# Half as many turned columns a chunk, and degrees summed by VectorE: a graph layer on one core

## The chip, the core and the metric

The kernel runs on one core of one Trainium2 chip. The time is the device time of one execution in microseconds (us). Engines are called as in the profile: PE is TensorE's matmul, PEld its weight load, DVE is VectorE, ACT is ScalarE, POOL is GpSimd, SP is SyncE (here it only issues DMAs).

## What is computed

A message-passing layer over a graph of 12500 nodes (48 features) and 400000 edges (32 features), the edges sorted by `dst`:

```
h   = relu(layernorm(x))
tmp = concatenate([h[dst], h[src], edge_attr], axis=1)
m   = relu(tmp @ W1 + b1) @ W2 + b2
out = x + segment_sum(m, dst)
```

The product with W1 is split by rows of W1: `A = h @ W1[:48] + b1` and `B = h @ W1[48:96]` are computed once for all nodes and become two tables in HBM, `tab_a` and `tab_b`; table B is also kept in SBUF turned over, `bt` (128 hidden values on the partitions, one column a node). An edge then needs `relu(A[dst] + B[src] + edge_attr @ W1[96:])`. W2 and b2 are applied after the sum over edges, so the sum carries two things a node: the summed hidden rows, and the node's degree (how many edges it has), by which b2 is multiplied.

## The kernel before, in words

`node_tables` makes the tables. `windows` then walks over 391 chunks of 1024 edges, each 8 tiles of 128 edges. Since edges are sorted, the destinations of a chunk lie in a window of 80 nodes. For chunk c:

- `prepare` (L338): SP loads 80 rows of table A (`rhs`, L344), the edge features (`lhs` rows 80 to 111, L349) and the destinations, spread over 80 partitions (`row`, L351). POOL gathers rows of table B by `src`, one indirect DMA for each tile of 128 edges (L358), into `gb`, a ring of 6 buffers: POOL may be up to six chunks ahead, and waits for `hid` of the chunk whose buffer it reuses. DVE compares destinations with the window's nodes: `lhs` (L365, 80 nodes by 1024 edges) and `hot` (L370, 128 edges by 8 times 80 nodes).
- `before` (L383): PE multiplies `lhs` by `rhs`, 8 products into `pre` in PSUM: A[dst] plus the part of the edge features.
- `columns` (L336): not all B rows are gathered. For 361 of the 390 full chunks the last tile's 128 rows are copied as columns out of `bt` into a tile `gt`, one instruction for each edge, its address from a register. DVE copies 59 columns a chunk and ACT 60, in parts (PARTS: 23, 20, 16 on DVE, 28, 32 on ACT), and each part's registers are loaded by one instruction (L300) that stands ahead of it. `turned` (L393): PE multiplies `gt` by the identity, which adds the turned tile to `pre`.
- `hidden`: DVE adds `gb` to `pre` (L401, 7 tiles, or 8 where none is turned); ACT applies relu (L403 for the turned tile straight from PSUM, L404 for the others).
- `fold` (L412): PE multiplies `hid` by `hot`, 8 products that accumulate the 80 nodes' sums in `p_g`; then 8 bf16 products of a matrix with one column of ones by the upper halves of `hot` (L417) accumulate the degrees.
- `add` (L431): DVE adds `p_g` to the segment's accumulator `seg`; every twelfth chunk begins a new segment (`segment_next`: two memsets L447 and a copy L449), and `segment_sum` and `segment_store` bring old segments through W2 (L457 to L459) to the output.

The order is written out by hand (the loop at the end of `windows`). In step c, PE does `before(c-1)`, `fold(c-2)`, `turned(c-1)`; DVE does the comparisons of c with three parts of columns, `hidden(c-1)`, then `add(c-2)`; ACT does a part of columns, the relus of c-1, and another part. Every engine works through its instructions in this order and waits on semaphores.

Of the kernel before, what the change touches and what calls it, by code (L numbers as in the profile page):

```python
# [11 lines left out]
ALU = mybir.AluOpType  # L12
# [46 lines left out]
BASE = 120  # L59

BT0 = 16512
SEG0 = 121952
# [3 lines left out]
SEG, NEXT, SEG2 = 124, 125, 126  # L66
PLACE0 = 127
WIDTH = 128
# [10 lines left out]
BYCOLS = tiles_of(COLS, PART)  # L79
EPS = 1e-5  # L80
# [151 lines left out]
def windows(nc, tc, gp, bt, ident, idx, x_t, tab_a, tab_b, dst, edge_t, w1, w2s, b2s, out_t):  # L232


    srci, rel, bw, wrow, last, ones = idx
    with ExitStack() as es:
# [5 lines left out]
        gtp = es.enter_context(tc.tile_pool(name="gtp", bufs=3))  # L242
# [81 lines left out]
        def columns(c, part):  # L324

            dve, first, _, _ = PARTS[part]
            copy = nc.vector.tensor_copy if dve else nc.scalar.copy
            for k, at in enumerate(regs.pop((c, part), [])):
                j, e = divmod((c - COLS) * PART + first + k, P)
                of = BYCOLS[j]  # L330
# [5 lines left out]
                copy(gts[of][:, e : e + 1], bt8[:, bass.ds(at, 4)].bitcast(F32))  # L336

        def prepare(c):  # L338
# [18 lines left out]
            for t in range(n - (c in BYCOLS)):  # L357
# [6 lines left out]

            nc.vector.tensor_scalar(  # L365
                lhs[:W, : n * P], row[:, : n * P], bw[:, c : c + 1], None, op0=ALU.is_equal,
            )
            columns(c, 0)
# [5 lines left out]
            load(c, 1)  # L374
            st[c].update(rhs=rhs, lhs=lhs, gb=gb, hot=hot)

        def before(c):
# [4 lines left out]
            for t in range(n):  # L382
                nc.tensor.matmul(  # L383
                    pre[:, t, :], s["lhs"][:K, t * P : (t + 1) * P], s["rhs"][:K, :],
                    start=True, stop=c not in BYCOLS or t < n - 1,
                )
            s["pre"], s["added"] = pre, n - (c in BYCOLS)

        def turned(c):

            if c in BYCOLS:
                s = st[c]
                nc.tensor.matmul(  # L393
                    s["pre"][:, s["n"] - 1, :], gts.pop(c), ident, start=False, stop=True
                )

        def hidden(c):
            s = st[c]
            n, m, pre = s["n"], s["added"], s["pre"]
            h = wp.tile([P, T, HID], F32, name="hid")  # L400
            nc.vector.tensor_add(h[:, :m, :], pre[:, :m, :], s["gb"][:, :m, :])  # L401
            if m < n:
                nc.scalar.activation(h[:, m, :], pre[:, m, :], AF.Relu)  # L403
            nc.scalar.activation(h[:, :m, :], h[:, :m, :], AF.Relu)  # L404
            s["h"] = h

        def fold(c):
# [7 lines left out]
            high = s["hot"].bitcast(BF16)  # L415
            for t in range(n):
                nc.tensor.matmul(  # L417
                    p_g[:, 1, :], ones, high[:, t, 1::2], start=t == 0, stop=t == n - 1
                )
# [45 lines left out]
        with tc.manual_schedule():  # L465
            for c in range(NCH + 2):
                if c < NCH:
                    prepare(c)
                if c >= NCH:
                    columns(c, 0)  # L470
                columns(c, 1)
                load(c, 2)
                columns(c, 2)
# [24 lines left out]
                load(c + 1, 3)  # L498
# [133 lines left out]
def tile_gnn_preln(  # L632
# [55 lines left out]
    ones = const.tile([P, P], BF16, name="ones")  # L688
    nc.gpsimd.memset(ones, 0.0)
    nc.gpsimd.memset(ones[:, :1], 1.0)  # L690
# [77 lines left out]
    with tc.If(outside == 0) as cmp:  # L768
        windows(nc, tc, gp, bt, ident, (srci, rel, bw, wrow, last, ones), x_t, tab_a, tab_b, dst16, edge_t,
# [71 lines left out]
```

## Time and profile before

| what | value |
|---|---|
| time, median of 3 runs | 4973.62 us (4969.75 to 4973.76) |
| the profiled execution's own time | 4973.7 us |
| its span, first to last instruction | 4972.0 us |
| mean granted TensorE clock | 0.644 |
| busy: PE, PEld, DVE, ACT, POOL | 65%, 58%, 59%, 59%, 54% |
| instructions in the span | 94216 |
| gathers on POOL | 2764 |
| columns copied by ACT, by DVE | 23280, 22928 |
| first and last `hid` addition on DVE | 159.3 us, 4959.4 us |

How to read the rows: in the groups of instructions, a row gives the line, engine, operation, what it writes and reads, its count, then busy time in all and the mean of one in ns, then the idle time of the engine just ahead of it and what ended that. In a timeline a row gives start and duration in us, and in brackets the idle time of the engine ahead of it and what ended it: "issue" is a wait for nothing that the profile shows, "remote" a wait that ended with an event from elsewhere that could not be told. "x15" are 15 instructions merged. Register loads are not counted as busy. 391 chunks end between 159.3 and 4959.4 us, about 12.3 us each.

### The profile page before, as it was taken

The numbers are of one execution on the slowest core, as the hardware profiler recorded it, in microseconds if no ns is written. First come the engines' busy times: TensorE is split into PE (matmuls) and PEld (weight loads), VectorE is DVE, ScalarE is ACT, GpSimd is POOL, SyncE is SP. The second block draws the span as 40 slices with busy tenths as digits, with TensorE's granted clock in tenths as the row PEclk, the third lists the DMA queues.
The fourth block names the chain that finished last, engine by engine and source line by source line (L and its number), as shares of the span: only waits on it lengthen the run. The fifth ranks groups of instructions, "written<-read, shape, count | busy, mean of one in ns | idle before, by whom it ended". The sixth has DMA issues, their size and how long they took to land.

```text
span 4972.0 us, 94216 instructions
## 1 busy us (share of the span) xinstructions
PE 3217.5 (65%) x16917; PEld 2903.8 (58%) x16917; DVE 2921.8 (59%) x24741; ACT 2925.2 (59%) x24107; POOL 2704.3 (54%) x2791
## 2 busy tenths in 40 slices
PE   6666766666666666666665666666666666666666
PEld 4556655555555555566565556565555655655555
DVE  4555555555566555556565555655555555555555
ACT  3456656655566556556566555656555556555565
POOL 5355555555555555555555555555555555555553
PEclk7666666666666666666666666666666666666666
DMA  3422222222222222222222222222222222222221
GB/s 128 134 65 73 69 69 67 69 64 72 69 69 67 69 65 74 68 68 68 68 66 71 69 69 67 69 69 69 67 69 67 69 69 68 69 69 67 69 68 49
DMA packets 192085, 353.66 MB, mean 71 GB/s; under 512 B 65282, under 2 KB 97428, under 8 KB 190196
## 3 DMA queue, kind: packets, MB, share of 16 engines
q0 software_dynamic: 88480, 181.34, 14.5%
q1 hardware_dynamic: 102736, 166.09, 11.2%
q14 instruction: 470, 3.85, 0.3%
q8 instruction: 139, 2.28, 0.2%
q10 hardware_dynamic: 260, 0.10, 0.0%
HBM read 327.81 MB, written 22.07 MB: 70 GB/s over the span
## 4 chain that ended last, share of the span: by engine, by line
issue 37%; DVE 24%; POOL 21%; ACT 8%; PE 3%; DVEq 3%; DMA 2%; another core or an unknown queue 1%; ACTq 1%; SPq 0%; POOLq 0%
POOL gb L358 21%; DVE gt L336 14%; ACT gt L336 7%; DVE hid L401 3%; DVE lhs L365 3%; DVEq L300 3%; DVE hot L370 2%; DMA gb<-tab_b,srci 1%; ACT hid L404 1%; PE p_g L412 1%; PE p_n L178 1%; PE pre L383 1%; ACTq L300 1%; DVE seg L431 1%
## 5 line engine op out<-in xcount | busy, mean ns | idle before, releaser
L358 POOL DMA_INDIRECT gb<-tab_b,srci x2764 | 2682.8, 971 | 2202.5 <-DVE hid L401 1438.1
L336 ACT COPY gt<-bt 128x1 f32 x23280 | 2476.5, 187 | 1843.6 <-issue 1817.5
L336 DVE COPY gt<-bt 128x1 f32 x22928 | 1708.5, 143 | 1715.5 <-issue 1634.7
L412 PE MATMUL p_g<-hot,hid 128*128 128x80 f32 x6250 | 1397.0, 415 | 1618.9 <-ACT hid L404 1409.7
L412 PEld LDWEIGHTS p_g<-hot,hid 128*128 128x128 f32 x6250 | 1315.0, 320 | 1702.2 <-ACT hid L404 1481.3
L383 PEld LDWEIGHTS pre<-rhs,lhs 112*128 112x128 f32 x6250 | 1155.9, 285 | 99.1 <-issue 85.9
L383 PE MATMUL pre<-rhs,lhs 112*128 112x128 f32 x6250 | 1177.3, 368 | 16.7 <-DVE lhs L365 16.7
L401 DVE TENSOR_TENSOR hid<-pre,gb 128x896 f32<-128x896 f32 (+1 forms) x391 | 426.7, 1091 | 7.8 <-issue 6.7
L404 ACT ACTIVATE hid<-hid 128x896 f32<-128x896 f32 (+1 forms) x391 | 369.9, 946 | 33.6 <-DVE hid L401 33.2
L393 PE MATMUL pre<-ident,gt 128*128 128x128 f32 x722 | 278.0, 488 | 64.3 <-remote 57.5
L365 DVE TENSOR_SCALAR lhs<-row,bw 80x1024 f32<-80x1024 int16 x391 | 310.5, 794 | 12.6 <-DMA row<-in_dst 7.6
L370 DVE TENSOR_TENSOR hot<-wnum,rel 128x640 f32<-128x640 f32 x391 | 315.9, 808 | 0.8 <-issue 0.7
L417 PEld LDWEIGHTS <-ones 128*128 128x128 bf16 x3125 | 292.8, 154 | 0.0
L417 PE MATMUL p_g<-hot,ones 128*128 128x80 bf16 x3125 | 284.5, 266 | 0.0
L431 DVE TENSOR_TENSOR seg<-seg,p_g 128x160 f32 x391 | 125.8, 322 | 196.1 <-DVE hid L401 185.1
L393 PEld LDWEIGHTS pre<-ident,gt 128*128 128x128 f32 x722 | 193.0, 327 | 70.2 <-remote 62.0
L403 ACT ACTIVATE hid<-pre 128x128 f32<-128x128 f32 x361 | 97.1, 269 | 71.2 <-DVE hid L401 68.7
L457 PE MATMUL p_f<-seg,w2s 128*48 128x512 f32 (+1 forms) x134 | 122.0, 1012 | 0.4 <-DVE seg L431 0.4
L458 PE MATMUL p_f<-seg,b2s 1*48 1x512 f32 (+1 forms) x134 | 101.9, 851 | 0.0
L458 PEld LDWEIGHTS p_f<-seg,b2s 1*48 1x48 f32 x134 | 13.6, 149 | 101.6 <-issue 101.6
L447 DVE MEMSET seg<- 128x944 f32 x64 | 54.1, 845 | 9.3
L459 DVE TENSOR_TENSOR xseg<-xseg,p_f 48x512 f32<-48x512 f32 (+1 forms) x67 | 44.8, 669 | 21.6 <-PE p_f L458 21.5
(66 smaller groups left out, 298.1 us busy)
## 6 DMA issues: line engine op xcount, KB each, us to landing
row<-in_dst SPq DMA_DIRECT2D x390, 160.0 KB
lhs<-in_edge_t SPq DMA_DIRECT2D x390, 128.0 KB
gb<-tab_b,srci POOLq DMA_INDIRECT x2764
rhs<-tab_a SPq DMA_DIRECT2D x391, 40.0 KB
xseg<-in_x_t SPq DMA_DIRECT2D x33, 192.0 KB
out_x<-xseg SPq DMA_DIRECT2D x33, 192.0 KB
tab_b<-tab SPq DMA_DIRECT2D x3, 1280.0 KB
tab_a<-tab SPq DMA_DIRECT2D x3, 1280.0 KB
```

The source lines that it names most:

```text
L300: got += nc.values_load_multi_w_load_instructions(last[c % P : c % P + 1, c // P, at + k : at + min(k + MOST, n)], engines=[engine], min_v ...
L336: copy(gts[of][:, e : e + 1], bt8[:, bass.ds(at, 4)].bitcast(F32))
L358: nc.gpsimd.indirect_dma_start(out=gb[:, t, :], out_offset=None, in_=tab_b[:, :], in_offset=bass.IndirectOffsetOnAxis(ap=srci[:, c * T + t ...
L365: nc.vector.tensor_scalar(lhs[:W, : n * P], row[:, : n * P], bw[:, c : c + 1], None, op0=ALU.is_equal,)
L370: nc.vector.tensor_tensor(hot[:, :n, :], wnum.unsqueeze(1).to_broadcast([P, n, W]), rel[:, c * T : c * T + n].unsqueeze(2).to_broadcast([P ...
L383: nc.tensor.matmul(pre[:, t, :], s["lhs"][:K, t * P : (t + 1) * P], s["rhs"][:K, :], start=True, stop=c not in BYCOLS or t < n - 1,)
L393: nc.tensor.matmul(s["pre"][:, s["n"] - 1, :], gts.pop(c), ident, start=False, stop=True)
L401: nc.vector.tensor_add(h[:, :m, :], pre[:, :m, :], s["gb"][:, :m, :])
L404: nc.scalar.activation(h[:, :m, :], h[:, :m, :], AF.Relu)
L412: nc.tensor.matmul(p_g[:, 0, :], s["h"][:, t, :], s["hot"][:, t, :], start=t == 0, stop=t == n - 1)
L417: nc.tensor.matmul(p_g[:, 1, :], ones, high[:, t, 1::2], start=t == 0, stop=t == n - 1)
L431: nc.vector.tensor_add(to, to, s["p_g"])
```

## The change

The number of columns goes from 119 to 63 a chunk: 31 on DVE (parts of 15 and 16) and 32 on ACT (16 and 16). So 191 tiles instead of 361 come out of `bt`, at most one a chunk still (the code can now also place two in a chunk, which does not occur with 63), and POOL's gathers go from 2764 to 2934. `gt` has 5 buffers instead of 3. The parts stand at other places of the step: the second DVE part comes after `hidden` and `add`, and its registers are loaded ahead of `add`. The degrees: DVE's comparison into `lhs` also writes the sum of its 1024 results for each of the 80 nodes into column 0 of a tile `deg` (three of them, otherwise zero), and PE turns that by one fp32 product with the identity, in place of the 8 bf16 products.

```
-    (True, 0, 23, 1), (True, 23, 20, 24), (True, 43, 16, 44),
-    (False, 59, 28, 60), (False, 87, 32, 88),
+    (True, 0, 15, 1),
+    (True, 15, 16, 16),
+    (False, 31, 16, 32),
+    (False, 47, 16, 48),
...
-        gtp = es.enter_context(tc.tile_pool(name="gtp", bufs=3))
+        gtp = es.enter_context(tc.tile_pool(name="gtp", bufs=5))
...
-            for t in range(n - (c in BYCOLS)):
+            for t in gathered_at(c):
...
+            deg = degs[c % 3]
             nc.vector.tensor_scalar(
-                lhs[:W, : n * P], row[:, : n * P], bw[:, c : c + 1], None, op0=ALU.is_equal,
-            )
+                lhs[:W, : n * P], row[:, : n * P], bw[:, c : c + 1], None,
+                op0=ALU.is_equal, op1=ALU.add, accum_out=deg[:, :1],
+            )
+            load(c, 0)
             columns(c, 0)
...
-            high = s["hot"].bitcast(BF16)
-            for t in range(n):
-                nc.tensor.matmul(
-                    p_g[:, 1, :], ones, high[:, t, 1::2], start=t == 0, stop=t == n - 1
-                )
+            nc.tensor.matmul(p_g[:, 1, :], s["deg"], ident[:W, :W], start=True, stop=True)
...
-                columns(c, 3)
+                columns(c, DVE_PARTS)
+                for part in range(DVE_PARTS + 1, BEHIND):
+                    load(c, part)
+                    columns(c, part)
                 if 0 <= c - 1 < NCH:
                     hidden(c - 1)
-                load(c + 1, 0)
-                load(c, 4)
-                columns(c, 4)
+                if DVE_PARTS > 1:
+                    load(c, DVE_PARTS - 1)
+                for part in range(BEHIND, len(PARTS)):
+                    load(c, part)
+                    columns(c, part)
+                load(c + 1, DVE_PARTS)
                 if 0 <= c - 2 < NCH:
                     add(c - 2)
                     if k == GQ - 1:
                         segment_next(g)
-                load(c + 1, 3)
+                if DVE_PARTS > 1:
+                    columns(c, DVE_PARTS - 1)
```

DVE, one chunk in the middle of the loop before, from one `hid` on; TENSOR_LOAD is the load of a part's registers, DMASW are the semaphores of POOL's gathers, DMAHW those of SP's loads:

```order
L401 TENSOR_TENSOR hid<-pre,gb 128x896 [waits DMASW4_49,DMASW3_49,DMASW5_49,DMASW2_49,DMASW6_49,DMASW0_49,DMASW7_49,PE_49,Activation_49]
L300 TENSOR_LOAD last
L431 TENSOR_TENSOR seg_659<-seg_659,p_g 128x2x80 [waits DVE_49]
L365 TENSOR_SCALAR lhs<-row,bw 80x1024 [waits DMAHW4_49]
L336 COPY gt<-bt 128x1 [waits Activation_49]
L336 COPY gt<-bt 128x1 x22
L370 TENSOR_TENSOR hot<-wnum,rel 128x640
L300 TENSOR_LOAD last
L336 COPY gt<-bt 128x1 x20
L300 TENSOR_LOAD last
L336 COPY gt<-bt 128x1 x16
```

DVE, the same stretch of the changed program, up to the next `hid`:

```order
L426 TENSOR_TENSOR hid<-pre,gb 128x896 [waits DMASW4_49,DMASW2_49,DMASW5_49,DMASW1_49,DMASW6_49,DMASW0_49,DMASW7_49,PE_49,Activation_49]
L317 TENSOR_LOAD last
L456 TENSOR_TENSOR seg_663<-seg_663,p_g 128x2x80 [waits DVE_49]
L352 COPY gt<-bt 128x1 x16
L382 TENSOR_SCALAR lhs,deg_90<-row,bw 80x1024 [waits DMAHW6_49,DMAHW1_49]
L317 TENSOR_LOAD last
L352 COPY gt<-bt 128x1 x15
L389 TENSOR_TENSOR hot<-wnum,rel 128x640
```

From one `hid` to the next there are 31 copies instead of 59 and two register loads instead of three; `lhs` stands behind 16 copies instead of directly behind `seg`, and between `hot` and the next `hid` no copies are left.

PE in the changed program, in the middle of the loop: two chunks, the second of which has a turned tile:

```order
L441 MATMUL p_g<-hot,hid 128x80 [waits PE_49,Activation_49]
L441 MATMUL p_g<-hot,hid 128x80 x7
L444 MATMUL p_g<-ident,deg_88 128x80
L401 MATMUL pre<-rhs_707,lhs 128x128 [waits DMAHW4_49,DMAHW5_49,DVE_49,PE_49]
L401 MATMUL pre<-rhs_707,lhs 128x128 x7
L441 MATMUL p_g<-hot,hid 128x80 [waits PE_49,Activation_49]
L441 MATMUL p_g<-hot,hid 128x80 x7
L444 MATMUL p_g<-ident,deg_90 128x80
L410 MATMUL pre<-ident,gt 128x128 [waits DVE_49]
```

Before, at the place of L444 stood eight pairs of a weight load and a product (L417), and the product with the identity (L393, now L410) followed in 361 chunks; now it follows in 191. A `hid` of a chunk without a turned tile waits for the products L401 of its chunk only; with one it waits for L410, which stands behind the `fold` of the chunk before.

More of the change, by code (lines that the diff above doesn't have):

```diff
@@ L373, in prepare @@
             )
-            load(c, 1)
-            st[c].update(rhs=rhs, lhs=lhs, gb=gb, hot=hot)
+            st[c].update(rhs=rhs, lhs=lhs, gb=gb, deg=deg, hot=hot)
         def before(c):
@@ L768, in tile_gnn_preln @@
     with tc.If(outside == 0) as cmp:
-        windows(nc, tc, gp, bt, ident, (srci, rel, bw, wrow, last, ones), x_t, tab_a, tab_b, dst16, edge_t,
+        windows(nc, tc, gp, bt, ident, (srci, rel, bw, wrow, last, degs), x_t, tab_a, tab_b, dst16, edge_t,
                 w1, w2s, b2s, out_t)
```

69 lines of the change are left out of this document (43 added, 26 removed).

## The prediction

> **What bounds the kernel now.** I read the page's engines and costliest groups first, then timelines of whole chunks, then start and end of the run. The page:
>
> ```profile
> span 4972.0 us, 94216 instructions
> PE 3217.5 (65%) x16917; PEld 2903.8 (58%) x16917; DVE 2921.8 (59%) x24741; ACT 2925.2 (59%) x24107; POOL 2704.3 (54%) x2791
> ...
> L358 POOL DMA_INDIRECT gb<-tab_b,srci x2764 | 2682.8, 971 | 2202.5 <-DVE hid L401 1438.1
> L336 ACT COPY gt<-bt 128x1 f32 x23280 | 2476.5, 187 | 1843.6 <-issue 1817.5
> L336 DVE COPY gt<-bt 128x1 f32 x22928 | 1708.5, 143 | 1715.5 <-issue 1634.7
> L412 PE MATMUL p_g<-hot,hid 128*128 128x80 f32 x6250 | 1397.0, 415 | 1618.9 <-ACT hid L404 1409.7
> ```
>
> No engine is full. PE waits for ACT, POOL for DVE's `hid` (1438 us), and DVE and ACT lose 1635 and 1818 us ahead of column copies to "issue", which names no culprit. A timeline of one chunk shows what that is:
>
> ```profile
> 2506.52 1.08 DVE L401 TENSOR_TENSOR hid<-pre,gb 128x896 f32<-128x896 f32 x1
> 2507.87 0.94 POOL L358 DMA_INDIRECT gb<-tab_b,srci  x1 [3.74 <-DVE hid L401]
> ...
> 2509.12 1.02 POOL L358 DMA_INDIRECT gb<-tab_b,srci  x1 [0.30 <-issue]
> 2509.25 1.46 DVE L336 COPY gt<-bt 128x1 f32 x23
> 2509.75 2.73 ACT L336 COPY gt<-bt 128x1 f32 x28 [0.86 <-issue]
> ...
> 2512.85 0.16 DVE L336 COPY gt<-bt 128x1 f32 x1 [0.28 <-issue]
> ...
> 2513.57 0.21 DVE L336 COPY gt<-bt 128x1 f32 x2 [0.56 <-issue]
> ...
> 2514.98 0.28 ACT L336 COPY gt<-bt 128x1 f32 x2 [0.52 <-issue]
> 2514.98 0.28 DVE L336 COPY gt<-bt 128x1 f32 x3 [1.20 <-issue]
> 2515.45 0.94 POOL L358 DMA_INDIRECT gb<-tab_b,srci  x1 [0.30 <-issue]
> ...
> 2517.87 1.00 DVE L336 COPY gt<-bt 128x1 f32 x15 [0.55 <-issue]
> 2517.87 2.23 ACT L336 COPY gt<-bt 128x1 f32 x23 [0.52 <-issue]
> 2518.28 0.33 SPq L344 DMA_DIRECT2D rhs<-tab_a  x1
> 2518.78 1.08 DVE L401 TENSOR_TENSOR hid<-pre,gb 128x896 f32<-128x896 f32 x1
> ...
> 2520.14 1.22 POOL L358 DMA_INDIRECT gb<-tab_b,srci  x1 [3.74 <-DVE hid L401]
> ```
>
> At first 23 copies take 1.46 us on DVE (63 ns each) and 28 take 2.73 us on ACT (98 ns). From about 2512.5 both engines go on only at common instants 0.71 us apart, one to three copies at each; at 2517.87 both run freely again, and only then do SP and `hid` proceed. I call this the **held stretch** and its end the release. It belongs to the gathers: they start 1.25 us apart, and the release comes 2517.87 - 2515.45 = 2.42 us after the start of the last. A chunk with eight gathers moves it by the same:
>
> ```profile
> 279.36 0.95 POOL L358 DMA_INDIRECT gb<-tab_b,srci  x1 [0.30 <-issue]
> ...
> 281.81 1.67 ACT L336 COPY gt<-bt 128x1 f32 x17 [1.12 <-issue]
> 281.94 1.09 DVE L401 TENSOR_TENSOR hid<-pre,gb 128x896 f32<-128x896 f32 x1 [1.31 <-issue]
> ```
>
> Here it is 2.45 us after. And after the last gather of all, with as many columns as ever, the chunks shrink (the first row is the first `hid` of the run):
>
> ```profile
> 159.29 1.22 DVE L401 TENSOR_TENSOR hid<-pre,gb 128x1024 f32<-128x1024 f32 x1
> ...
> 4915.47 0.95 POOL L358 DMA_INDIRECT gb<-tab_b,srci  x1 [0.30 <-issue]
> ...
> 4919.81 1.22 DVE L401 TENSOR_TENSOR hid<-pre,gb 128x1024 f32<-128x1024 f32 x1
> ...
> 4927.49 1.08 DVE L401 TENSOR_TENSOR hid<-pre,gb 128x896 f32<-128x896 f32 x1
> ```
>
> 7.68 us instead of 12.26 (2506.52 to 2518.78). So columns alone do not set the pace. What the stretch does to work that needs several engines in turn is seen at the start, where POOL fills its six buffers without a pause, up to 106.9 us, while the tables are made:
>
> ```profile
> 79.19 1.35 PEld L178 LDWEIGHTS p_n<-wa,ht 97*128 97x128 f32 x4 [2.21 <-issue]
> ...
> 88.05 0.59 ACT L187 COPY tab<-p_n 128x512 f32<-128x512 f32 x1 [12.47 <-remote]
> 88.69 1.35 PEld L178 LDWEIGHTS p_n<-wa,ht 97*128 97x128 f32 x4 [8.14 <-issue]
> ...
> 99.26 0.69 DVE L185 COPY tab<-p_n 128x512 f32<-128x512 f32 x1 [20.18 <-remote]
> ...
> 105.91 0.95 POOL L358 DMA_INDIRECT gb<-tab_b,srci  x1 [0.30 <-issue]
> ```
>
> PE's products with the weights loaded from 79.19 on (done near 81 us) reach ACT at 88.05, 7 us late; the next set, done near 91, reaches DVE at 99.26. In a held stretch word of PE's work arrives late, mostly at the release. The main loop agrees (PE's wait for the columns ends at a release):
>
> ```profile
> 2617.74 2.33 ACT L336 COPY gt<-bt 128x1 f32 x24 [0.51 <-issue]
> ...
> 2617.80 0.80 PE L393 MATMUL pre<-ident,gt 128*128 128x128 f32 x2 [6.48 <-remote]
> ```
>
> So a chunk of before is a ring: release, 0.91 us of leftover copies (2517.87 to 2518.78), `hid`, 1.36 us to the first gather (2518.78 to 2520.14), six steps of 1.25, 2.42 to the release: 0.91 + 1.36 + 7.50 + 2.42 = 12.19 us, against 12.26 seen. **The bound is POOL's run with its held stretch, plus what DVE still does between release and `hid`.**
>
> **The change part by part.** Rows for the prices:
>
> ```profile
> L447 DVE MEMSET seg<- 128x944 f32 x64 | 54.1, 845 | 9.3
> ...
> L401 DVE TENSOR_TENSOR hid<-pre,gb 128x896 f32<-128x896 f32 (+1 forms) x391 | 426.7, 1091 | 7.8 <-issue 6.7
> ...
> L365 DVE TENSOR_SCALAR lhs<-row,bw 80x1024 f32<-80x1024 int16 x391 | 310.5, 794 | 12.6 <-DMA row<-in_dst 7.6
> ...
> L417 PE MATMUL p_g<-hot,ones 128*128 128x80 bf16 x3125 | 284.5, 266 | 0.0
> ```
>
> Columns: 28 fewer a chunk on each engine save 28 x 63 ns = 1.8 us on DVE and 28 x 98 ns = 2.7 us on ACT where they run freely. On the path lies only what stood behind the release. By the order DVE had 66 instructions a chunk (59 copies, 3 register loads, `lhs`, `hot`, `hid`, `seg`) and now has 37. I take it that all copies are done when the release comes, so release to `hid` shrinks from 0.91 to the semaphore's way alone: 0.4 us (2518.28 - 2517.87 = 0.41, SP's first DMA behind the same release). A gain of 0.5 us; bounds 0 and 0.9.
>
> Gathers: 2934 against 2764, 7.50 a chunk instead of 7.07: 0.43 x 1.25 = +0.54 us a chunk, 170 x 1.25 = 212 us in all if each run still starts behind a `hid`.
>
> Degrees on PE: 284.5 us / 391 = 0.73 us a chunk go, one fp32 product comes. Its weight load and product are like those of L393 (two passes in 0.80 us, quoted above), so 0 to 0.8 us. PE's idle 1619 us ahead of L412 hide either; I count 0.
>
> Degrees on DVE: `lhs` now also accumulates. It takes 794 ns for 1024 elements a partition; `hid` takes 1091 ns for 896. At `hid`'s pace 1024 elements cost 1.25 us, and the sum may need a small operation like a copy (143 ns). So 0.8 to 1.4 us; I take 1.3, nearest to `hid`'s row: +0.5 us a chunk, behind `hid`, covered by the wait for the next release (DVE's free work from `hid` on: 1.1 + 0.3 + 1.0 + 1.3 + 0.9 + 0.8, about 5.5 us with the way between them). Without that cover it costs 385 x 0.5 = 190 us. The Trainium skill speaks to this: the page "SBUF — State Buffer", section "Who interferes with whom", says that a `tensor_scalar` that also writes out its accumulator is not among the operations that can take the two-port modes. By that page `lhs` loses its doubled rate, which the upper bound above already holds; no run here shows the accumulating form.
>
> The turned chunks: with 191 of 390 turned, about every second chunk's `hid` needs no L410, so it does not wait for `fold` of the chunk before. This is what I think decides. Behind a release at 0 `hid(c-1)` starts at 0.4, the next gathers at 1.76, and DVE gets to `hid(c)` at about 6. In the chunk above, copies ran freely until about 2512.5, 4.6 us behind the first gather; so 6 us is within a few instructions of the free time. If chunk c has no turned tile, its products L401 ran early and nothing holds `hid(c)`: it runs inside the stretch, and at the next release POOL starts at once, without the 0.4 + 1.36. A turned chunk's `hid` needs `fold` and L410, whose word comes with a release.
>
> So chunks go in pairs: 0.4 + 1.36 for the first run, 0.25 for the second, two tails of 2.42, and 15 gathers less two ends, 13 x 1.25 = 16.25: **23.10 us a pair, 11.55 a chunk.** New segments (two memsets of 845 ns, 32 times) fall into DVE's slack. Larger `gt` rings and the moved parts take nothing from the path: SP's loads run three chunks ahead.
>
> The sum, against the profiled execution's 4973.7 us (the median of 4973.62 is the same): the first `hid` is at 159.3 and stays. The 385 chunks up to the last gather give 385 x 11.55 = 4447. Behind `hid` at 4919.81 come 53.9 us of six ungathered chunks; fewer copies make it about 50. Together 159 + 4447 + 50 = **4656, say 4660 us.**
>
> **The rivals.** First, longer runs: word of the early `hid(c)` gets out of the stretch before POOL finishes its chunk. POOL then does 15 gathers in one run: 0.4 + 1.36 + 14 x 1.25 + 2.42 = 21.68 a pair, 385 x 10.84 + 209 = 4380. For it: `hid(c)` is near the start of the held stretch. Against: a release at the start of the run took 7 us and more.
>
> Second, gathers back to back: DVE and ACT with half the copies no longer hold POOL at all: 7.50 x 1.25 = 9.38 a chunk, 385 x 9.38 + 209 = 3820. The Trainium skill would have it so: the page "SBUF — State Buffer", section "Who interferes with whom", states that DMA never contends with a compute engine and that PE and ACT never wait on anyone. By that rule fewer copies would simply leave POOL as the bound; here the trace disagrees, with copies at 0.71 us instants under gathers and 7.68 against 12.26 us a chunk. Against it stands the start of the run, where unbroken gathers made steps of 10 us.
>
> Third, slower: no `hid` gets ahead, since the stretch catches DVE before it (after about 4.6 us of gathers, when 15 copies, `hot` and `hid` are still to do). Then each chunk pays all: 0.4 + 1.36 + 6.50 x 1.25 + 2.42 = 12.31, and new segments still cost 32 x 1.7 = 54 us: 159 + 385 x 12.31 + 54 + 50 = 5002. The extra gathers (+0.54) eat what the leftover copies gave back (-0.5). It decides where DVE reaches `hid(c)` later than about 6 us behind the release; `lhs` at 1.4 us pushes that way.
>
> That the change does not do what it says: the order shows 31 copies between two `hid` and 7 or 8 gathers, so I give this nothing.
>
> **How the numbers follow.** Pairs 0.40; longer runs 0.23; back to back 0.09; each chunk alone 0.28, of which I put 0.20 above 4984 us, 0.05 within 0.2% and 0.03 below. (0.2%, 10 us, is about what a measurement of this kernel can tell from no change.) Faster: 0.40 + 0.23 + 0.09 + 0.03 = 0.75; same 0.05; slower 0.20. The range reaches from 50 us below the longer runs (4330) to 5050, the third rival with 0.1 us a chunk more; left out are the back-to-back case and the far ends of the others, near 0.2. The likeliest case's own range is 4570 to 4760 (`lhs`, 0.25 and 0.4 us, each off by their size).
>
> **What the profile after would show.** Pairs: `hid` at alternating distances, one of each two behind a release and one inside the held stretch; POOL's waits for `hid` about half of 381; 7- and 8-gather runs with a gap of about 1.7 us between the two of a pair and 3.3 between pairs. Longer runs: 15 gathers at 1.25 us. Back to back: POOL near all its span. Alone: 381 waits as before. `lhs` should stand near 1.25 us, with DVE idle ahead of `hid`. Wrong would be the whole account if the held stretch vanished with fewer copies, or if copies were slow without gathers.

## The result, and the profile after

The changed kernel took 4986.68 us (median of 14 runs) against 4973.53 us before (14 runs): a ratio of **1.0023, 95% interval 1.0015 to 1.0032**. The forecast was 4660 us. The time lies inside the forecast's range, but it is slightly slower, where faster was forecast.

The experiments came in five sets, each on one chip with its own runs of the kernel before (D and E on the same chip). In three of them the kernel before took about 3630 us instead of 4900 to 4974, and the traces taken in these sets show no held stretch ("the hold" from here on) in any kernel:

| set | kernel before, us | changed kernel, ratio | held stretch |
|---|---|---|---|
| first (the result) | 4973.5 | 1.0023 (1.0015 to 1.0032) | yes |
| A | 3627.8 | not run | no |
| B | 4961.4 | 1.0010 (1.0000 to 1.0020) | yes |
| C | 4902.2 | not run | yes |
| D | 3631.5 | 1.0332 (1.0315 to 1.0350) | no |
| E | 3628.8 | not run | no |

So each ratio below is to the kernel before of its own set. With the hold the change costs 0.1 to 0.2%; without it, it costs 3.3%.

The page of the changed kernel (first set), rows that answer to those of before:

```profile
span 4988.6 us, 67352 instructions
PE 2965.4 (59%) x14234; PEld 2653.0 (53%) x14234; DVE 2250.1 (45%) x14235; ACT 1953.8 (39%) x13073; POOL 2803.0 (56%) x2962
...
L374 POOL DMA_INDIRECT gb<-tab_b,srci x2934 | 2781.4, 948 | 2128.4 <-DVE seg L456 1055.6
L352 ACT COPY gt<-bt 128x1 f32 x12416 | 1497.5, 188 | 2227.8 <-issue 2206.5
...
L456 DVE TENSOR_TENSOR seg<-seg,p_g 128x160 f32 x391 | 123.3, 315 | 1609.9 <-remote 1366.0
...
L382 DVE TENSOR_SCALAR_CACHE_REDUCE lhs<-row,bw 80x1024 f32<-80x1024 int16 x391 | 495.0, 1266 | 57.9 <-issue 48.2
...
L444 PE MATMUL p_g<-ident,deg 80*128 80x80 f32 x782 | 218.1, 359 | 173.2 <-issue 171.0
```

More than a quarter of all instructions are gone, and DVE and ACT have 670 and 970 us less to do, yet ACT loses more time to "issue" than before (2207 us against 1818), and a new wait of 1366 us stands ahead of DVE's `seg`, whose row was, before:

```profile
L431 DVE TENSOR_TENSOR seg<-seg,p_g 128x160 f32 x391 | 125.8, 322 | 196.1 <-DVE hid L401 185.1
```

A timeline of one pair of chunks in the same run shows where (start, duration; in brackets the idle time ahead and what ended it):

```profile
2657.17 0.64 DVE L352 COPY gt<-bt 128x1 f32 x9 [1.24 <-issue]
...
2657.72 0.81 DVE L389 TENSOR_TENSOR hot<-wnum,rel 128x640 f32<-128x640 f32 x1
...
2658.45 1.08 DVE L426 TENSOR_TENSOR hid<-pre,gb 128x896 f32<-128x896 f32 x1
...
2659.80 0.94 POOL L374 DMA_INDIRECT gb<-tab_b,srci  x1 [5.48 <-DVE seg L456]
...
2663.26 0.39 PE L444 MATMUL p_g<-ident,deg 80*128 80x80 f32 x2
...
2663.49 1.21 DVE L426 TENSOR_TENSOR hid<-pre,gb 128x1024 f32<-128x1024 f32 x1
2663.55 0.94 POOL L374 DMA_INDIRECT gb<-tab_b,srci  x1 [0.30 <-issue]
2664.11 0.19 ACT L352 COPY gt<-bt 128x1 f32 x1 [0.53 <-issue]
...
2667.66 1.06 ACT L433 ACTIVATE hid<-hid 128x1024 f32<-128x1024 f32 x1 [0.44 <-issue]
...
2672.72 3.49 PE L441 MATMUL p_g<-hot,hid 128*128 128x80 f32 x15 [7.25 <-remote]
...
2676.91 0.32 DVE L456 TENSOR_TENSOR seg<-seg,p_g 128x160 f32 x1 [12.21 <-remote]
...
2677.15 1.05 DVE L352 COPY gt<-bt 128x1 f32 x16
2677.29 0.94 POOL L374 DMA_INDIRECT gb<-tab_b,srci  x1 [0.30 <-issue]
...
2681.08 0.76 DVE L352 COPY gt<-bt 128x1 f32 x11 [1.23 <-issue]
...
2681.76 0.81 DVE L389 TENSOR_TENSOR hot<-wnum,rel 128x640 f32<-128x640 f32 x1
...
2682.49 1.08 DVE L426 TENSOR_TENSOR hid<-pre,gb 128x896 f32<-128x896 f32 x1
...
2683.84 0.94 POOL L374 DMA_INDIRECT gb<-tab_b,srci  x1 [5.61 <-DVE seg L456]
```

The chunk without a turned tile has its `hid` 5.04 us behind the other one (2663.49), and POOL goes on without a pause (0.30 us): 15 gathers in one run, 2659.80 to 2677.29. Split where POOL stood idle for more than 1 us, the 2934 gathers make 217 runs, and 169 of them are such fifteens. In the meantime DVE stands at `seg` for 12.21 us. This `seg` adds the chunk before, whose last PE product (L444) was done at 2663.65, but the trace has the update of PE's semaphore at 2676.88, 13 us later. The fold of the chunk without a turned tile waits in the same way: ACT's relu ended at 2668.72, and PE goes on at 2672.72. The release comes at 2681.08, **3.79 us** after the last gather's start, and DVE then still has 11 copies and `hot` to do, 1.41 us to `hid` (2682.49); at the release ahead of this pair (2657.17) it was **1.28 us**. The sum is 1.28 + 1.35 + 14 x 1.25 + 3.79 = 23.9 us a pair, 12.0 a chunk. The mean of all chunks is 12.35 (first `hid` 158.3, last 4976.1, 390 steps); it holds the new segments and the chunks that go alone as well. Over the whole run the tail after the last gather is 3.81 us (median of 156 runs of 15 in which ACT's copies show the release) and release to `hid` 1.49; in the kernel before they were 2.39 and 0.85 (356 runs of 7).

Set against before: 12.31 us a chunk were 7.07 gathers of 1.25 us (8.84) and 3.47 us between them; 12.35 us are 7.50 gathers (9.38) and 2.97 us between them. **Half a microsecond saved, half a microsecond of gathers added.**

### The profile page after: what moved, and what is told of

Read it like the earlier page. It is cut to its first block, busy times and chain, and to the rows that moved or that the text cites. A ratio compares the mean times of both kernels' runs of the same rounds, so it can differ in the third digit from the quotient of the medians.

```text
span 4988.6 us, 67352 instructions
## 1 busy us (share of the span) xinstructions
PE 2965.4 (59%) x14234; PEld 2653.0 (53%) x14234; DVE 2250.1 (45%) x14235; ACT 1953.8 (39%) x13073; POOL 2803.0 (56%) x2962
## 4 chain that ended last, share of the span: by engine, by line
PE 37%; another core or an unknown queue 26%; issue 17%; DVE 13%; DVEq 2%; ACT 1%; ACTq 0%; DMA 0%; POOL 0%
PE p_g L441 16%; PE pre L401 14%; DVE gt L352 5%; DVE lhs L382 3%; PE p_g L444 2%; DVE hot L389 2%; DVEq L317 2%; DVE hid L426 2%; PE pre L410 2%; PE p_f L483 2%; PE p_f L482 1%; DVE seg L456 1%; ACT gt L352 1%; ACTq L317 0%
## 5 line engine op out<-in xcount | busy, mean ns | idle before, releaser
L374 POOL DMA_INDIRECT gb<-tab_b,srci x2934 | 2781.4, 948 | 2128.4 <-DVE seg L456 1055.6
L352 ACT COPY gt<-bt 128x1 f32 x12416 | 1497.5, 188 | 2227.8 <-issue 2206.5
L441 PE MATMUL p_g<-hot,hid 128*128 128x80 f32 x6250 | 1259.1, 379 | 1442.2 <-remote 915.6
L441 PEld LDWEIGHTS p_g<-hot,hid 128*128 128x128 f32 x6250 | 1195.4, 291 | 1459.5 <-remote 948.2
L401 PE MATMUL pre<-rhs,lhs 112*128 112x128 f32 x6250 | 1231.7, 377 | 112.3 <-issue 81.6
L401 PEld LDWEIGHTS pre<-rhs,lhs 112*128 112x128 f32 x6250 | 1172.1, 287 | 221.4 <-issue 199.8
L352 DVE COPY gt<-bt 128x1 f32 x12032 | 858.1, 142 | 597.9 <-issue 591.3
L382 DVE TENSOR_SCALAR_CACHE_REDUCE lhs<-row,bw 80x1024 f32<-80x1024 int16 x391 | 495.0, 1266 | 57.9 <-issue 48.2
L444 PE MATMUL p_g<-ident,deg 80*128 80x80 f32 x782 | 218.1, 359 | 173.2 <-issue 171.0
L444 PEld LDWEIGHTS p_g<-ident,deg 80*128 80x128 f32 x782 | 183.0, 278 | 199.6 <-issue 199.4
L410 PE MATMUL pre<-ident,gt 128*128 128x128 f32 x382 | 141.9, 456 | 232.7 <-remote 128.0
L410 PEld LDWEIGHTS pre<-ident,gt 128*128 128x128 f32 x382 | 99.6, 306 | 272.3 <-issue 148.1
```

Of the source, the lines that this page charges most:

```text
L374: nc.gpsimd.indirect_dma_start(out=gb[:, t, :], out_offset=None, in_=tab_b[:, :], in_offset=bass.IndirectOffsetOnAxis(ap=srci[:, c * T + t ...
L382: nc.vector.tensor_scalar(lhs[:W, : n * P], row[:, : n * P], bw[:, c : c + 1], None, op0=ALU.is_equal, op1=ALU.add, accum_out=deg[:, :1],)
L401: nc.tensor.matmul(pre[:, t, :], s["lhs"][:K, t * P : (t + 1) * P], s["rhs"][:K, :], start=True, stop=t not in turned_at(c),)
L410: nc.tensor.matmul(st[c]["pre"][:, t, :], gts.pop(j), ident, start=False, stop=True)
L441: nc.tensor.matmul(p_g[:, 0, :], s["h"][:, t, :], s["hot"][:, t, :], start=t == 0, stop=t == n - 1)
L444: nc.tensor.matmul(p_g[:, 1, :], s["deg"], ident[:W, :W], start=True, stop=True)
```

## The experiments

Theory at the start: in a pair the long run makes release and `hid` late, and the two sizes above are where the forecast gain went. Rivals: the degrees' part (`lhs`, the fp32 product) ate it; or the hold is not what sets the time.

**No gathers (A and D).** The gathers are left out behind the sixth chunk; later chunks add those old rows.

```
-            gb = gp.tile([P, T, HID], F32, name="gb")
-            for t in gathered_at(c):
+            if c < 6:
+                gbs.append(gp.tile([P, T, HID], F32, name="gb"))
+            gb = gbs[c % 6]
+            for t in range(T) if c < 6 else ():
```

> The changed kernel with gathers for its first six chunks only; all later chunks add those same gathered rows, so the sums of edges are left wrong for them. Theory (the gathers hold the other engines up, columns alone do not): without gathers a chunk takes what DVE's own work takes, 5.0 us (the distance of the early hid in the changed kernel), to 7.7 us (the ungathered chunks at the end of the kernel before): 160 + 391 x 5.0 to 7.7 = 2100 to 3200 us, and no copy on a 0.71 us instant. Rival (DVE, ACT and PE are slow by themselves, by columns, lhs or the degree product): above 4000 us.

2344.31 us (one run), inside the theory's range; DVE, busy 92% of the span, sets the time. But set A had no hold to take away, so this doesn't tell. Once more, for a set with the hold:

> The changed kernel with gathers for its first six chunks only (the sums of the later chunks' edges use those rows), once more, for the case that the kernel before stands near 4960 us. Theory (the gathers hold the engines up, and nothing else does): 2344 us again in spite of it. Rival (a chip on which the engines' word is slow by itself): clearly above, 3000 us and more.

2344.7 us (one run), but set D had no hold either. That the gathers cause it where it occurs thus rests on the traces (7.68 us a chunk after the last gather), not on this run.

**All gathered (A and C).** No turned tile, no copy, 3125 gathers.

```
-BYCOLS = tiles_of(COLS, PART)
+BYCOLS = []
```

> The changed kernel with no turned tile and no column copy at all: every tile is gathered, 3125 gathers. Theory (any unbroken run of gathers makes word between engines late, with or without copies): 8 gathers x 1.25 = 10.0 us a chunk, plus the 2.5 to 3.1 us a chunk that runs of 8 and of 15 lose in the changed kernel: 12.5 to 13.1 us, 209 + 385 x 12.5 to 13.1 = 5020 to 5250 us. Rival (the column copies fill what lies between the engines, and their absence frees it): POOL back to back at 10.0 us a chunk, 209 + 385 x 10.0 = 4060 us, and word from PE within 1 us.

Set A: 3974.74 us (one run), ratio 1.096, 10.0 us a chunk: POOL never pauses. That is the rival's figure, but without a hold the set tells neither. Set C, with the hold:

> The changed kernel with every tile gathered and no column copy, once more. If the kernel before stands near 4960 us: theory (unbroken gathers hold the word of every engine, copies or not) 12.5 to 13.1 us a chunk, 5020 to 5250 us; rival (the number of instructions is what the stretch holds, so that without 63 copies a chunk all get through): gathers back to back, 10.0 us a chunk, 4060 us or less. If it stands near 3628 us: 3975 us again.

5108.9 us (one run), ratio 1.042, 12.7 us a chunk, as the theory had it. Its timeline, inside a run of 24 gathers and at its end:

```profile
2531.27 0.94 POOL L374 DMA_INDIRECT gb<-tab_b,srci  x1 [0.30 <-issue]
2532.10 0.37 PE L401 MATMUL pre<-rhs,lhs 112*128 112x128 f32 x1 [2.32 <-issue]
...
2532.80 0.29 PEld L441 LDWEIGHTS p_g<-hot,hid 128*128 128x128 f32 x1 [1.82 <-issue]
2533.50 0.29 PE L441 MATMUL p_g<-hot,hid 128*128 128x80 f32 x1 [1.02 <-issue]
...
2534.18 0.29 PEld L441 LDWEIGHTS p_g<-hot,hid 128*128 128x128 f32 x1 [1.10 <-issue]
...
2542.50 0.94 POOL L374 DMA_INDIRECT gb<-tab_b,srci  x1 [0.30 <-issue]
...
2547.48 1.79 PE L441 MATMUL p_g<-hot,hid 128*128 128x80 f32 x8 [0.41 <-issue]
```

With ACT busy 9% of the span and DVE 29% it is now PE that goes on by single instructions at instants 0.70 us apart, so the hold does not need the copies. The release is 4.98 us after the start of the last gather of 24. So the tail grew with the length of the run: 2.42 us after 7 gathers, 3.79 after 15, 4.98 after 24. The gathers' own data are not late: in all three timelines the last packet of the last gather ends 2.1 to 2.2 us after its start.

**The changed and the old kernel again (B, D).**

> The changed kernel, unaltered, beside the kernel before on one chip. Two theories, since the set of runs before had the kernel before at 3628 us instead of 4974. Theory 1 (the held stretch is nothing that the program makes: some chips or times have it, others don't): if the kernel before stands near 3628 us here, gathers go back to back and the changed kernel is POOL's 2934 gathers, 3868 us as with the degrees on PE, 6 to 7% slower; if before stands near 4974 us, the changed kernel is at 4987 again. Theory 2 (the changed kernel brings the held stretch on itself, the others don't): about 4987 us whatever before does.

> The kernel before, unaltered, for its profile. Theory 1: near 3628 us, POOL's 2764 gathers start 1.25 to 1.3 us apart nearly without a pause (2764 x 1.25 = 3455 us and about 170 us around them), no copies on 0.71 us instants; or near 4974 us with the held stretch as in the first profile. Theory 2: 4974 us.

Set B: 4964.84 us, 1.0010 (1.0000 to 1.0020); before 4962.35 us (one run), with the hold. Theory 1: the hold goes with the set, not with the program. Set D:

> The changed kernel, unaltered, as the measure for the others of this set. If the kernel before stands near 3628 us: 2934 gathers back to back, 3868 us, 6.6% slower. If it stands at 4900 to 4974 us: 0.1 to 0.3% above it.

3751.15 us, 1.0332 (1.0315 to 1.0350); 117 us below what was expected (on that below). Its page and timeline:

```profile
span 3750.1 us, 67352 instructions
...
POOL 61%; issue 28%; DMA 4%; DVE 1%; PE 1%; DVEq 0%; ACT 0%; POOLq 0%; ACTq 0%
...
L374 POOL DMA_INDIRECT gb<-tab_b,srci x2934 | 2776.1, 946 | 921.2 <-issue 870.3
L441 PE MATMUL p_g<-hot,hid 128*128 128x80 f32 x6250 | 1173.8, 366 | 956.3 <-ACT hid L433 947.1
L352 ACT COPY gt<-bt 128x1 f32 x12416 | 1228.6, 187 | 40.5 <-issue 13.8
```

```profile
2505.37 0.94 ACT L433 ACTIVATE hid<-hid 128x896 f32<-128x896 f32 x1
...
2506.30 3.17 ACT L352 COPY gt<-bt 128x1 f32 x32
...
2506.37 2.58 PE L441 MATMUL p_g<-hot,hid 128*128 128x80 f32 x16 [2.27 <-ACT hid L433]
2506.39 0.94 POOL L374 DMA_INDIRECT gb<-tab_b,srci  x1 [0.30 <-issue]
```

Under gathers that never pause, 32 copies take their 3.17 us, and PE follows the relu at once. POOL with its 0.30 us between gathers is nearly the whole chain: 2934 x 1.25 = 3667 us, and 84 around it. The gathers themselves are the same as with the hold (946 against 948 ns).

**The columns alone (A and C).** Degrees by PE's bf16 products, 63 columns. The memset of `ones` stands in POOL's queue here, so its first gather starts at 90.6 instead of 51 us.

```
-                lhs[:W, : n * P], row[:, : n * P], bw[:, c : c + 1], None,
-                op0=ALU.is_equal, op1=ALU.add, accum_out=deg[:, :1],
+                lhs[:W, : n * P], row[:, : n * P], bw[:, c : c + 1], None, op0=ALU.is_equal,
...
-            nc.tensor.matmul(p_g[:, 1, :], s["deg"], ident[:W, :W], start=True, stop=True)
+            high = s["hot"].bitcast(BF16)
+            for t in range(n):
+                nc.tensor.matmul(
+                    p_g[:, 1, :], ones, high[:, t, 1::2], start=t == 0, stop=t == n - 1
+                )
```

> The changed kernel with the degrees by PE's eight bf16 products again and lhs without its sum: the columns' part of the change alone. Theory (the gain was lost to the late release and what stands behind it; lhs's 0.47 us and the fp32 degree product are hidden in the run of 15 gathers): 4940 to 5030 us. Rival (the accumulating lhs, 1.27 instead of 0.79 us, and the fp32 product, in DVE's and PE's way, ate it): 385 x 0.47 = 180 us faster or more, 4800 us or less.

> The columns' part of the change alone (degrees by PE's bf16 products again), once more, for the case that the kernel before stands near 4960 to 4974 us. Theory (in held stretches DVE's free time is on the path, so that lhs's sum costs what it takes): lhs falls from 1.27 to 0.79 us a chunk, as the degrees' part alone cost 162 us: 4980 - 391 x 0.41 to 0.48 = 4790 to 4830 us, 3% faster than before. Rival (in a run of 15 gathers lhs is hidden, and what costs is the late release): 4940 to 5000 us. If the kernel before stands near 3628 us: 3868 us again, by both.

Set A: 3868.24 us, 1.0666 (1.0648 to 1.0683). Set C, with the hold: 4940.66 us, **1.0073 (1.0056 to 1.0090)**. Set A had no hold, so neither theory was told there. In set C the theory fails by its sign. The rival's 4940 to 5000 us was meant for a kernel before of 4960 to 4974; as a ratio it is about 0.99 to 1.01, and it holds. The changed kernel itself was not run in set C; its ratios in the other sets with the hold are 1.0010 and 1.0023. By these, which cross sets, the columns alone are some 0.5% slower than the whole change, so the degrees' part is not what ate the gain. POOL's row shows one side of it, `deg_on_pe_2`:

```profile
L377 POOL DMA_INDIRECT gb<-tab_b,srci x2934 | 2880.0, 982 | 1932.9 <-issue 818.5 <-DVE hid L428 588.5 <-DVE seg L462 499.9
```

A gather takes 982 ns with the plain `lhs` and 948 ns with the accumulating one; before it was 971. 34 ns x 2934 = 100 us. In the trace of before (set B) a long gather lies beside `lhs`:

```profile
2538.84 1.25 POOL L358 DMA_INDIRECT gb<-tab_b,srci  x1 [3.73 <-DVE hid L401]
2538.99 0.32 DVE L431 TENSOR_TENSOR seg<-seg,p_g 128x160 f32 x1 [0.42 <-DVE hid L401]
2539.23 0.74 DVE L365 TENSOR_SCALAR lhs<-row,bw 80x1024 f32<-80x1024 int16 x1
```

1.25 us instead of 0.94, over the time of `lhs`. In the first trace of before all 347 gathers above 1.0 us (up to 1.47) overlap a `lhs`; in `deg_alone` below, the same kernel with the accumulating form, one gather of 2764 is above 1.0 us. The Trainium skill has a rule that fits, in "SBUF — State Buffer", section "Who interferes with whom": a plain `tensor_scalar` can take the two-port mode, and whichever of DVE and GpSimd comes first then locks the other out for its whole instruction, while the form that writes out its accumulator cannot take that mode. The rows agree: with that form the mean gather takes 944 to 952 ns in every run that gathers throughout. The other side is the end of a run: with the plain `lhs` it is 4.74 us from the last gather of 15 to `hid` (median), against 5.31 in the changed kernel (first set, so again across sets). The accumulating form shortens the gathers and lengthens the way to `hid`; by these numbers the two nearly balance. I had used this rule in the prediction for DVE's rate only, and missed what it does for POOL. For the 117 us by which set D's changed kernel fell below the 3868 us, this (2859.5 - 2776.1 = 83 us of POOL's busy time by the two pages) and the late start (39 us) come to 122.

**The degrees alone (B).** The kernel before, 119 columns, with the accumulating `lhs`.

```
-                lhs[:W, : n * P], row[:, : n * P], bw[:, c : c + 1], None, op0=ALU.is_equal,
+                lhs[:W, : n * P], row[:, : n * P], bw[:, c : c + 1], None,
+                op0=ALU.is_equal, op1=ALU.add, accum_out=degs[c % 3][:, :1],
```

> The kernel before with only the degrees' part of the change: 119 columns as ever, lhs accumulates and one fp32 product replaces eight bf16 ones. Theory (POOL's gathers set the time and hide both): within 0.3% of the kernel before. Rival (lhs's 0.47 us a chunk is on the path): 391 x 0.47 = 185 us slower; or PE's 0.7 us a chunk was: some 270 us faster.

5123.02 us, **1.0334 (1.0317 to 1.0351)**, 162 us slower: the rival. In the order of before, DVE's time up to the hold is full:

```profile
2536.52 0.95 POOL L363 DMA_INDIRECT gb<-tab_b,srci  x1 [0.30 <-issue]
...
2538.96 1.24 DVE L341 COPY gt<-bt 128x1 f32 x19 [1.20 <-issue]
...
2540.12 1.08 DVE L407 TENSOR_TENSOR hid<-pre,gb 128x896 f32<-128x896 f32 x1
```

19 copies are left at the release, and `hid` starts 3.60 us after the last gather's start; in the prediction's chunk of before it was 3.33 (medians over 356 runs of 7 gathers 3.57 and, in set B's trace of before, 3.22). What `lhs` takes longer ahead of the hold, copies do behind the release. The late start of POOL (90.4 us here too) plays no part: the first `hid` is at 153.0 us, against 157.5 in set B's trace of before.

**Chunks alone (A and C).** L401's products behind the fold, so no `hid` runs ahead.

```
+                if 0 <= c - 2 < NCH:
+                    fold(c - 2)
                 if 0 <= c - 1 < NCH:
                     before(c - 1)
-                if 0 <= c - 2 < NCH:
-                    fold(c - 2)
```

> The changed kernel with PE's products of chunk c-1 (L401) put behind the fold of chunk c-2, so that no hid can run ahead of the fold. Theory (chunks go in pairs because every second hid gets ahead, and a pair saves one release): runs of 7 and 8 gathers alone, at what such runs take in the changed kernel, 12.25 and 12.87 us, with a new segment every twelfth chunk: 12.6 to 13.2 us a chunk, 209 + 385 x 12.6 to 13.2 = 5060 to 5290 us. Rival (a chunk loses the same 3 us whatever the length of the run): 4987 us within 0.5%, with runs of 7 and 8.

> The changed kernel with L401's products behind the fold, once more. If the kernel before stands near 4960 us: runs of 7 and 8 gathers alone, 12.6 to 13.2 us a chunk by the theory that pairs save a release, 5060 to 5290 us; 4980 us by the rival that a chunk loses the same 3 us whatever the length of its run. If it stands near 3628 us: 4320 us again.

Set A: 4319.94 us, 1.1905 (1.1885 to 1.1925); the products behind the fold make POOL wait there, which neither theory had looked at. Set C: 5042.57 us, ratio 1.029 (one run), 2.7% above the changed kernel's 1.001 to 1.002; the theory's range is 1.02 to 1.07 as a ratio. How much of this is the pairs isn't separated, since set A shows that the new order costs time without a hold too. By the trace a run of 7 and one of 8 take 11.67 and 12.99 us (medians), 24.66 together, against 24.19 for a run of 15 in the changed kernel. Single runs show the forecast's sizes:

```profile
2533.05 0.94 POOL L374 DMA_INDIRECT gb<-tab_b,srci  x1 [0.30 <-issue]
2535.84 0.33 SPq L360 DMA_DIRECT2D rhs<-tab_a  x1
2535.91 1.22 DVE L426 TENSOR_TENSOR hid<-pre,gb 128x1024 f32<-128x1024 f32 x1 [7.58 <-issue]
```

`hid` comes 2.86 us after the last gather, with no copy left; the forecast had 2.42 + 0.4.

**The addition late (C).** `seg` behind `hot`, so DVE needn't wait for PE's word ahead of its copies.

```
+                if 0 <= c - 3 < NCH:
+                    add(c - 3)
...
                 g, k = group(c - 2)
...
-                if 0 <= c - 2 < NCH:
+                if c == NCH + 1:
                     add(c - 2)
```

> The changed kernel with DVE's addition into seg (L456) moved from right behind a hid to behind hot of the next step, ahead of the next hid, so that DVE does its 31 copies, lhs and hot without waiting for the fold of the chunk before. Theory (in a run of 15 gathers DVE stands at seg for 7 to 12 us, and its copies and hot are then still to do behind the release, 1.3 us ahead of hid): release to hid falls to about 0.8 us, 0.25 us a chunk less, 4980 - 96 = 4880 us, down to 4800 us if PE's L410 comes earlier too. Rival (PE's own late passes set hid, not DVE's leftovers): 4960 to 5000 us. If the kernel before stands near 3628 us: 3868 us within 0.5%.

4905.09 us, 1.0008 (0.9998 to 1.0018): no gain to speak of against the changed kernel's 1.0010 and 1.0023 (not run in this set), where 2% was expected; the theory that the order of DVE's work sets the late `hid` falls. The wait at `seg` is gone (5 us in all), but DVE now loses 1373 us to "issue" ahead of its copies, against 591 in the changed kernel:

```profile
2498.57 1.27 DVE L382 TENSOR_SCALAR_CACHE_REDUCE lhs<-row,bw 80x1024 f32<-80x1024 int16 x1 [4.79 <-issue]
...
2499.83 0.94 POOL L374 DMA_INDIRECT gb<-tab_b,srci  x1 [0.30 <-issue]
...
2503.46 0.58 DVE L352 COPY gt<-bt 128x1 f32 x8 [0.55 <-issue]
...
2503.95 0.81 DVE L389 TENSOR_TENSOR hot<-wnum,rel 128x640 f32<-128x640 f32 x1
...
2504.91 1.08 DVE L426 TENSOR_TENSOR hid<-pre,gb 128x896 f32<-128x896 f32 x1
```

The release is 3.63 us after the last gather and `hid` 1.45 us behind it, as in the changed kernel.

**More columns (B).** 126 a chunk in the changed order: PARTS of 31, 32, 31, 32.

> The changed kernel with 126 columns a chunk (31, 32 on DVE, 31, 32 on ACT) instead of 63: 382 tiles from the columns, 2743 gathers, one turned tile in nearly each chunk. Theory (the time is the number of gathers, as long as DVE and ACT keep up): where before stands at 3628 us, 21 gathers fewer than before, 3628 - 26 = 3600 us; where it stands at 4974 us, a ring of 12.1 us a chunk, 4870 to 4950 us. Rival (DVE or ACT becomes the bound: some 63 copies, lhs at 1.27, hot, hid and two register loads of 32 numbers a chunk): 10 us a chunk and more, 4000 us or more where before stands at 3628.

5721.09 us, **1.1541 (1.1508 to 1.1573)**, 14.2 us a chunk: the theory fails. The rival, for which no time had been given with the hold, has the kind of bound right: the page's chain is ACT 44% and issue 47%. From the last gather of 7 to `hid` it takes 4.98 us (median), against 3.22 before; with 63 copies on each engine the hold leaves more copies over than the 21 gathers fewer can pay.

**Fewer columns in the old order (D and E).** 103: PARTS of 19, 16, 16 and 26, 26.

> The kernel before with 103 columns a chunk instead of 119 (19, 16, 16 on DVE, 26, 26 on ACT), its order and degrees as they were: 313 turned tiles, 2812 gathers. Theory (the copies left over at the release, 0.91 us ahead of hid, are on the path, and nearly every chunk still has 7 gathers): 8 copies fewer on each engine take 0.4 to 0.5 us a chunk off, 48 gathers more cost 60 us: 385 x 0.45 - 60 = 110 us faster than the kernel before, 2.3%. Rival (the leftovers are only waiting for PE's word): 60 us slower, 1.2%. If the kernel before stands near 3628 us: 48 x 1.25 = 60 us slower, 3690 us.

> The kernel before with 103 columns a chunk, once more, for the case that the kernel before stands near 4900 to 4974 us. Theory (the copies left over at the release are on the path of the kernel before): 385 x 0.45 - 60 = 110 us faster, ratio 0.978. Rival (the leftovers only wait for PE's word): ratio 1.012. If the kernel before stands near 3630 us: 1.012 again.

1.0117 (1.0100 to 1.0134) and 1.0124 (1.0106 to 1.0142), as expected without the hold; neither set had it, so what 103 columns do under it stays open.

**The fold in bf16 (D and E).** `hot` and the relu's output in bf16, 16 PE instructions fewer a chunk.

```
-            hot = wp.tile([P, T, W], F32, name="hot")
+            hot = wp.tile([P, T, W], BF16, name="hot")
...
+            hb = wp.tile([P, T, HID], BF16, name="hidb")
...
-            nc.scalar.activation(added(h, to), added(h, to), AF.Relu)
+            nc.scalar.activation(added(hb, to), added(h, to), AF.Relu)
```

> The changed kernel with hot and the relu's output in bf16, so that the fold is 8 weight loads and 8 products a chunk instead of 16 and 16 (the hidden rows are rounded to bf16 before the sum). Theory (in the run of 15 gathers PE goes on by one instruction each 0.70 us, and its fold, degree product and L410 set hid and the release's 3.8 us): fewer of them let L410 come early; release after the last gather falls from 3.8 to about 2.5 us, release to hid from 1.3 to 1.0 or less: 0.6 to 0.8 us a chunk, 230 to 310 us under the changed kernel of the same set. Rival (DVE's and ACT's work behind the release is what counts; PE is idle half its time): within 0.7% of the changed kernel. If the kernel before stands near 3628 us: no change, 3870 us.

> The changed kernel with the fold in bf16, once more, for the case that the kernel before stands near 4900 to 4974 us (the changed kernel then at 1.001 to 1.002 of it). Theory (in the run of 15 gathers PE's fold, degree product and L410 go on one instruction each 0.70 us and set the late release and hid): 16 PE instructions fewer a chunk, 230 to 310 us off, ratio to the kernel before 0.94 to 0.955. Rival (DVE's and ACT's work behind the release counts): ratio 0.995 to 1.01. If the kernel before stands near 3630 us: 1.032 again.

1.0318 (1.0301 to 1.0336) and 1.0324 (1.0305 to 1.0342), the same as the changed kernel without the hold. Whether PE's instructions set the late release of the long runs **stays open**, since no set with the hold came to this kernel. No version tried beats the kernel before by more than can be measured.

## Why the prediction was wrong, point by point

- **The ring and the held stretch** were read rightly for the set on record, and in three later sets they didn't exist. The one profile of before could not tell that.
- **Release to `hid`, 0.91 to 0.4 us:** it fits the runs of one chunk in `fold_first_2` (2.86 us from the last gather, tail and all), and is wrong for runs of 15: 1.28 to 1.41 us.
- **Gathers, +0.54 us a chunk:** right with the hold. Without it the 170 gathers cost 120 us, not 212; the shorter gathers (971 ns with the plain `lhs`, 946 with the other, x 2764 = 69 us) would account for most of the rest.
- **Degrees on PE, counted 0:** L444 takes 2 x 359 ns a chunk, inside the bounds.
- **`lhs` 1.3 us, covered:** the size is right (1.266 + 0.079 us). That it is covered in the changed order isn't shown: with the plain form `hid` comes about half a microsecond earlier after the last gather (4.74 against 5.31 us). The price named for the uncovered case, 190 us, was 162 in the old order. Missed: the accumulating form frees POOL, 34 ns a gather.
- **Pairs:** right that every second `hid` runs early (5.04 us behind the other); POOL waits on DVE 215 times, where "about half of 381" was forecast; the two rows below hold 212 of them. (The row with `seg` is a wait for `hid` too: in the timeline `hid` ends 0.27 us ahead of the gather at 2659.80, as before, and `seg` only 0.04.)

```profile
POOL gb L374 <- DVE seg L456: 1055.6, 178, 12.9
...
POOL gb L374 <- DVE hid L426: 198.9, 34, 51.6
```

- **The step that failed** is "all copies are done when the release comes", with 0.4 us from release to `hid`: 9 to 11 copies and `hot` were left, and it took 1.28 to 1.41 us in the pair shown (median of the whole run 1.49). Against the likeliest case's 23.10 us a pair that is +0.88, and the pair shown took 23.92. The other terms came out even by luck: two runs with "two tails of 2.42" were forecast, 0.25 + 4.84 + 16.25 = 21.34 us, and one run of 15 with one tail of 3.79 came, 17.5 + 3.79 = 21.29. So the form of the first rival came true, since the early `hid`'s word did get out; its price, 21.68 us, took the tail and the leftovers of a short run for those of a long one (+1.37 and +0.88).
- **New segments, put at nothing** ("DVE's slack"): a run of 15 in which one begins takes 26.66 us to the next run, the others 24.49 (means of 27 and 142), 2.2 us each. With these, with the 46 chunks that go alone (12.57 us each) and with the slower pairs, 23.9 us becomes the mean of 24.7 (2 x 12.35), and all of the gain is gone.
- **What was not foreseen in a held run of 17 us:** part of the two chunks' work doesn't get done in it; it is moved behind the release. That much is shown. That the tail grows with the run (2.42, 3.79, 4.98 us) is shown too; why it does is not.
- **The slower rival** (5002 us) came close to the measured 4987 by luck: its mechanism, no `hid` ahead, is that of `fold_first_2`, 2.9% slower than before.
- **Back to back**, given 0.09, is what the changed kernel does without the hold: 9.29 us a chunk (9.38 forecast), 3751 us. The reason given, half the copies, is not the one: without the hold 103 columns go back to back as well. The Trainium skill's rule ("SBUF — State Buffer", "Who interferes with whom") is that DMA never contends with a compute engine and that PE and ACT never wait on anyone. The sets without the hold agree with it: ACT's copies have a mean of 187 ns both under unbroken gathers (`after_3`) and with none (`no_gathers`). In the sets with the hold PE waits under gathers even with no copies; whether SBUF has any part in that no run here shows.

## What to carry to other kernels

When a wait is removed and two short runs become one long one, price the long run's end anew: what was measured behind a short run isn't what stands behind a long one. A chunk's cost is best split into what is counted (gathers x 1.25 us) and what lies between, for before and after alike; here it shows at once that +0.54 met -0.50. And before a mechanism is optimized for, find out whether it is there on another chip: here the ratio of one change is 1.002 with it and 1.033 without.

## What the hardware showed that was not expected

- The held stretch is there or not by the set: 4902, 4961, 4974 us or 3628, 3629, 3632 us for one kernel, with gathers of 946 to 948 ns both ways in the changed one. The cause is not settled. Every one of these runs has a traced span on record, so none tells whether the hold is there when no trace is taken.
- Where it is, engines run freely at first. Counted in the traces from a run's first gather to the first of several starts 0.70 us apart (medians, all engines): 145 instructions in 4.3 us (changed kernel, runs of 15), 137 in 5.7 us (before, runs of 7), 163 in 8.5 us (all gathered, runs of 24), 98 in 5.0 us (`cols126`, runs of 7). So it is neither a fixed time nor a fixed number of instructions; what sets it is open. From then on instructions start at instants 0.70 to 0.71 us apart, and an engine's word can be 13 us late.
- A plain comparison into `lhs` (0.74 to 0.79 us) lengthens a gather beside it from 0.94 to up to 1.47 us; with the accumulating form (1.27 us) it doesn't. Of the changed kernel's 2934 gathers 21 still take more than 1.0 us, each beside the memsets and the copy of a new segment.
